# Turned squares of probabilities: sixteen SBUF-to-SBUF transfers, or four writes and one read through device memory

## The chip, the cores and the metric

One core of a Trainium2 chip. The time is the device time of one execution in microseconds (us), median of three runs. A core has a matrix engine (TensorE, in the profile PE, its weight loads PEld), a vector engine (VectorE, DVE), an activation engine (ScalarE, ACT), a general one (GpSimd, POOL), a queue engine that here only issues transfers (SyncE, SP), and 16 DMA engines that carry the transfers. Each engine works through its own instructions in order; semaphores order them against each other. SBUF is the on-chip memory of 128 partitions, PSUM the accumulator memory of TensorE, and device memory (DRAM in the code) lies off the core.

## The reference

Eight samples of 512 tokens with 512 features are normalised. One branch is a selective state-space scan, the other a gated feed-forward part whose gate is modulated by a causal attention of 16 heads of 32 numbers. What the change touches is the attention:

```python
q = (x @ Wq.T).reshape(b, s, H, HD)
k = (x @ Wk.T).reshape(b, s, H, HD)
v = (x @ Wv.T).reshape(b, s, H, HD)
scores = jnp.einsum('bqhd,bkhd->bhqk', q, k) / np.sqrt(HD)
scores = jnp.where(causal, scores, jnp.finfo(scores.dtype).min)
probs = jax.nn.softmax(scores, axis=-1)
out = jnp.einsum('bhqk,bkhd->bqhd', probs, v).reshape(b, s, d)
attn = out @ Wo.T
mod = MOD_SCALE * jnp.tanh(attn @ A)
gate_pre = h @ W_in_base.T + mod * (h @ A) @ B
...
x = x + s * g
```

`s` is the scan branch, `g` the silu of the feed-forward branch. Attention is used only through `attn @ A`, 16 numbers a token, so the kernel folds `Wv`, `Wo` and `A` into one matrix and gives every head 16 "values" plus a column of ones for the softmax's denominator.

## The kernel before

The kernel has two stages. The first, from the start to about 905 us, does the attention of all eight samples and, at its end, the convolutions of sample 0. The second does the scan, the feed-forward part and the projections; it is most of the time, and the change leaves it alone.

**Waves.** The attention goes in 32 waves: 8 samples times 4 groups of 4 heads. In the code a wave is `cur = (b, hg)`, the ones before are `prev`, `prev2`. A wave has four blocks of 128 queries, `qt` = 0 to 3, taken in the order 2, 1, 0, 3. Block `qt` sees `qt + 1` blocks of 128 keys.

**Steps of a block.** `scores` multiplies queries and keys into PSUM (line 1139, and the mask at 1144). `maxima` takes the row maxima on VectorE (1153). `exps` writes the exponentials to SBUF on ScalarE (1161). The product with the values needs the keys on the partitions, so the probabilities have to be turned. VectorE turns squares of 32 x 32 in place (`turn_blocks`, line 1180): blocks 0 to 2 go into the tile `ta` (128 x 4 x 6 x 128), block 3 into `tb` (128 x 4 x 4 x 128). Both have one buffer. After that every square is turned in itself, but still stands in the wrong block of 32 partitions.

**Moves.** `move_blocks` (1185) puts the squares in place: part (a, k) of `ta`, 32 partitions `a` and the column block `k`, goes to partitions `k` and column block `a` of `pta`; the same from `tb` to `ptb`. That is 16 transfers of 32 rows for each tile, issued by SyncE (1193). `pta` and `ptb` have one buffer each too.

**Products.** `attend` (1201, its matmuls at 1210) multiplies `pta` or `ptb` with the values into PSUM, and its `evict` copies the result to `o_sb`. `divide` turns it back on TensorE (1230) and divides by the denominator on VectorE. `modulation` closes a sample.

**What sets the order.** The kernel schedules by hand: each engine's order is the order in which the program issues. For the attention it is a string of words, one for a wave (1273). `S2`, `R2`, `E2` are scores, maxima and exponentials of block 2; `T2` turns it; `U3` turns block 3 of the wave before; `A` moves `ta` of this wave, `B` moves `tb` of the wave before; `a` and `e` are the products of the moved `ta` and `tb`, `O` the division; `q` and `k` are the projections of the next wave, `x`, `z`, `s`, `n`, `b`, `w`, `m` steps of the next sample (turning, values, statistics, normalising, weighing, modulation). A word with `>` is the eviction of the step with that letter. `ORDER_CONV` is for the last waves, in which `c` and `d` are convolutions of sample 0, and `ORDER_END` for the last. Behind the waves there is a tail, in which parts of the second stage (`run_part`) alternate with the last products.

**Other transfers on SyncE in this stage.** The loads of the next sample but one (`load_x`, 799, four at once), the store of the turned input (`scr_x`, 1069), constants in the first waves, and from the sixth wave before the end the weights of the convolutions (`load_win`, 218) and the stores of their results (`scr_c`, 259). GpSimd has its own queue: the row of normalising factors goes to device memory and back (979, 980), `hT` is stored (1089), the modulation is stored (1264).

Of the kernel before, what the change touches and what calls it, by code (L numbers as in the profile page):

```python
# [10 lines left out]
F32 = mybir.dt.float32  # L11
# [7 lines left out]
P = 128  # L19
# [4 lines left out]
TT = S // P  # L24
# [12 lines left out]
QD = 32  # L37
# [3 lines left out]
def mamba_gated_ffn_kernel(  # L41
# [22 lines left out]
    nc = tc.nc  # L64

    const = ctx.enter_context(tc.tile_pool(name="const", bufs=1))
    dram = ctx.enter_context(tc.tile_pool(name="scratch", bufs=1, space=DRAM))
# [6 lines left out]
    scr_c = [dram.tile([DI, S], F32, tag=f"scr_c{b}", name=f"scr_c{b}") for b in range(NB)]  # L74
    scr_r = [dram.tile([S], F32, tag=f"scr_r{b}", name=f"scr_r{b}") for b in range(NB)]
    scr_a = dram.tile([NS, DI], F32, tag="scr_a", name="scr_a")

    ident = const.tile([P, P], F32, tag="ident", name="ident")
    make_identity(nc, ident)
# [705 lines left out]
    with ExitStack() as c1:  # L785
# [53 lines left out]
        for i in range(2):  # L839
            z = wa.tile([P, TT, HG, 4, 2 * R], F32, tag=f"z{i}", name=f"z{i}")  # L840
# [344 lines left out]
        def move_blocks(b, hg, nm):  # L1185

            t = probs.pop((b, hg, nm))
            n = t.shape[2]
            to = pp.tile([P, 4, n, P], F32, tag=f"pt{nm}", name=f"pt{nm}_{b}_{hg}", bufs=1)
            for d in range(4):  # L1190
                for a in range(4):
                    k = (a + d) % 4
                    nc.sync.dma_start(to[ts(k, QD), a], t[ts(a, QD), k])  # L1193
            moved[b, hg, nm] = to

        PARTS = {
# [4 lines left out]
        def attend(b, hg, nm):  # L1201

            ps = bank(f"o_ps_{b}_{hg}_{nm}")
            t = moved.pop((b, hg, nm))
            steps = PARTS[nm]
            base = 0 if nm == "a" else (TT - 1) * P
            for s, (kt, qt, n, slot, by) in enumerate(steps):
                for h in range(4):
                    rhs = t[:, :, slot : slot + (n - 1) * by + 1 : by, ts(h, QD)]
                    nc.tensor.matmul(  # L1210
                        ps[ts(h, HD), qt * P - base : (qt + n) * P - base],
                        lhsT=zs[b % 2][:, kt, hg, h, :],
                        rhs=rhs.rearrange("p a n i -> p n a i"), start=(s == 0),
                        stop=(s == len(steps) - 1),
                    )

            def evict():
                if nm == "a":
                    outs[b, hg] = pp.tile([P, S], F32, tag="o_sb", name=f"o_{b}_{hg}", bufs=1)
                w = (TT - 1) * P if nm == "a" else P  # L1220
                nc.scalar.copy(outs[b, hg][:, base : base + w], ps[:, :w])

            return evict
# [24 lines left out]
        def modulation(b):  # L1248
# [22 lines left out]


        ORDER = (
            "S2 R2 U3 B E2 k s O x S1 k> R1 O> E1 x> T2 x a x> S0 a> R0 E0 T1 z z> "
            "T0 A z z> x x> b S3 R3 E3 q s b b e x q> s e> x> n b w m M"
        )
        ORDER_CONV = (
            "S2 R2 U3 B E2 d3 k O S1 d4 k> R1 O> E1 T2 c a c1 S0 a> R0 E0 c2 z z> T1 "
            "T0 A c3 z z> c4 S3 R3 E3 q d q> e d1 e> m w d2 M"
        )  # L1280
        ORDER_END = (
            "S2 R2 U3 B E2 d3 O S1 d4 R1 O> E1 T2 P a S0 a> R0 E0 P1 T1 T0 A S3 R3 E3 "
            "e 1 e> O O>"
        )

        def started(parts):
# [25 lines left out]
        def in_spare(fn, *args):  # L1312

            i = spare["n"] = spare.get("n", -1) + 1
            pair = ps_s.tile([P, 2, 512], F32, tag="s", name=f"s_spare_{i}")
            banks["special"] = lambda name: pair[:, 0, :]
            r = fn(*args)
            banks["special"] = None
            return r
# [15 lines left out]
            return [f for _, f in in_spare(started, sizes[i])]  # L1335

        items = [(b, hg) for b in range(NB) for hg in range(HG)]
        ends, late, divided = {}, {}, set()
        weigh_first()
        for g in range(len(items)):  # L1340
            cur = items[g]
            prev = items[g - 1] if g else None
            prev2 = items[g - 2] if g > 1 else None
            prev3 = items[g - 3] if g > 2 else None
            b, hg = cur
            n = b + 1
            ahead = items[g + 1] if g + 1 < len(items) else None
            todo = {k: [] for k in "bnxzsw"}
            if n < NB:
                if hg == 0:  # L1350
                    todo["b"], ends[n] = statistics(n)
                elif hg == 1:
                    todo["s"] = ends[n]
                    todo["n"] = [
                        lambda: [normalise(n, tt, nc.gpsimd) for tt in range(TT)]
                    ]
                elif hg == 2:
                    if n + 1 < NB:
                        load_x(n + 1)
                    todo["x"] = [lambda kt=kt: turn(n, kt) for kt in range(KT)]  # L1360
                    todo["w"] = [lambda: weigh(n)]
                else:
                    todo["z"] = [lambda tt=tt: values(n, tt) for tt in range(2)]
            if hg == 0 and b:
                todo["z"] = [lambda tt=tt: values(b, tt) for tt in (2, 3)]

            convs = g - (len(items) - 5)
            order = ORDER_CONV if convs >= 0 else ORDER
            if ahead is None:
                order = ORDER_END  # L1370
            open_, slot = {}, -1
            for w in order.split():
                kind, q = w[0], int(w[1]) if w[1:].isdigit() else None
                if kind == "S":
                    open_["R", q], open_["E", q] = scores(b, hg, q)
                    slot += 1
                elif kind in "RE":
                    open_.pop((kind, q))()
                elif kind == "T":
                    turn_blocks(*cur, q)  # L1380
                elif kind == "U":
                    if prev:
                        turn_blocks(*prev, q)
                elif w == "A":
                    move_blocks(*cur, "a")
                elif w == "B":
                    if prev:
                        move_blocks(*prev, "b")
                elif w in ("a", "e"):
                    if prev:  # L1390
                        late[w] = attend(*prev, "a" if w == "a" else "b")
                elif w in ("q", "k"):
                    late[w] = query_key(*ahead, w)
                    if w == "q" and g == len(items) - 6:
                        load_xn(0)
                        for d in range(3):
                            load_win(0, d)
                elif w == "O":
                    of = prev2 if prev2 not in divided else prev
                    if of:  # L1400
                        divided.add(of)
                        late["O"] = divide(*of)
                elif w == "m":
                    if prev2 and prev2[1] == HG - 1:
                        late["M"] = modulation(prev2[0])
                elif w == "M":
                    if "M" in late:
                        late.pop("M")()
                elif kind in "cd" and len(w) == 1:
                    late[kind] = convolution(2 * convs + (kind == "d"))  # L1410
                elif kind in "cd":
                    if late.get(kind):
                        late[kind].pop(0)()
                elif w == "P":
                    late["P"] = step_of_time(0)
                elif w == "P1":
                    for f in late["P"]:
                        f()
                elif w == "1":
                    late["P"] = step_of_time(1)  # L1420
                elif w[1:] == ">":
                    if w[0] in late:
                        late.pop(w[0])()
                elif todo.get(w):
                    f = todo[w].pop(0)()
                    if w in "xz":
                        late[w] = f
                if kind == "E" and g == 0:
                    for f, *i in folds[slot]:
                        f(*i)  # L1430
                if kind == "E" and (b, hg, slot) in const_steps:
                    const_steps[b, hg, slot]()
            if g == 0:
                for tt in range(TT):
                    values(0, tt)()
            assert not any(todo.values()), todo


        last = items[-1]
# [3 lines left out]
            f()  # L1443
        state["wait"] = True
        banks["second"] = None
        evict = in_spare(attend, *last, "a")
        run_part()
        evict()
        for i in (2, 3, 4):
            for f in step_of_time(i):  # L1450
                f()
# [41 lines left out]
    for b in range(NB):  # L1493
# [6 lines left out]
        for s in range(STEPS):  # L1500
            k = b * STEPS + s
# [107 lines left out]
```

## Time and profile before

| what | us |
|---|---|
| median of three runs | 3203.05 (3201.35 to 3204.26) |
| the profiled execution, its time | 3203.12 |
| its span, first to last instruction | 3201.3 |
| PE busy in the span | 2993.1 |
| DVE busy | 2517.0 |
| POOL busy | 1977.2 |
| ACT busy | 1266.6 |

The mean granted clock of TensorE is 0.96. The page also cuts the span into 40 slices of 80 us; a digit is the busy share in tenths, for PEclk the granted clock in tenths, for DMA the mean share of the 16 DMA engines.

```profile
PE 8677877779799999999999999999999999999999
...
DVE 5455654556669998997998899889879988998885
...
PEclk9788988889899999999999999999999999999999
DMA 4555555555567878787978877787778788787974
```

The first eleven digits are the attention stage: PE is mostly at six to eight tenths and its clock below full, DVE at about half, the DMA engines at about half. In the remaining 29 PE is at nine tenths or more.

How the page is read: a group of instructions has its source line, engine, operation, output and input tiles and count, then busy time and the mean of one, then the idle time before it with what ended it. PE's ends are modelled. Who waited for whom is inferred from semaphores. "SPq" is SyncE's queue of issuing instructions, which isn't counted as an engine's busy time. A DMA packet is one contiguous row of a transfer, and each DMA engine that took part adds a packet of 4 bytes that counts the transfer's semaphore up.

### The profile page before, as it was taken

Reading aid. Unit: us, or ns where it says so; the run is one execution under the profiler, and the core shown is the slowest. Engines: PE = TensorE matmul, PEld = TensorE weight load, DVE = VectorE, ACT = ScalarE, POOL = GpSimd, SP = SyncE. Lnnn points to the kernel's source line nnn. Section 1 sums busy time; section 2 is a strip of 40 time slices with the busy share of each in tenths; the row PEclk is TensorE's granted clock in tenths of the full one; section 3 lists DMA queues with packets and bytes.
Section 4 is the critical chain, followed back from the end, with each engine's and each line's share of the span. In section 5 each row is a group of like instructions: output and inputs, shape, how many; then the busy total and the mean of one; then the engine's idle time right before and its main releaser. Section 6 shows DMA issues by size and latency. Waiting matters only on the chain.

```text
span 3201.3 us, 35722 instructions
## 1 busy us (share of the span) xinstructions
PE 2993.1 (93%) x11956; PEld 1301.3 (41%) x11956; DVE 2517.0 (79%) x2858; ACT 1266.6 (40%) x2224; POOL 1977.2 (62%) x924
## 2 busy tenths in 40 slices
PE   8677877779799999999999999999999999999999
PEld 5333443334343344344434443443444344434444
DVE  5455654556669998997998899889879988998885
ACT  4343443434334443433443334334334433443432
POOL 2321122121058887887777787777778787788885
PEclk9788988889899999999999999999999999999999
DMA  4555555555567878787978877787778788787974
GB/s 145 140 130 131 138 150 142 125 133 162 164 181 207 204 208 227 206 206 185 243 181 217 214 202 199 200 228 200 197 194 226 191 222 207 198 207 186 232 187 120
DMA packets 344905, 595.13 MB, mean 186 GB/s; under 512 B 44749, under 2 KB 176333, under 8 KB 340116
## 3 DMA queue, kind: packets, MB, share of 16 engines
q1 hardware_dynamic: 338528, 576.35, 69.6%
q0 software_dynamic: 2192, 10.50, 1.1%
q10 hardware_dynamic: 4004, 6.01, 0.8%
q8 instruction: 96, 1.57, 0.2%
q14 instruction: 85, 0.70, 0.1%
HBM read 466.04 MB, written 42.77 MB: 159 GB/s over the span
## 4 chain that ended last, share of the span: by engine, by line
PE 79%; SPq 9%; DVE 4%; DMA 4%; POOL 2%; issue 2%; ACT 1%; DVEq 0%; ACTq 0%; POOLq 0%
PE ps_gu L298 27%; PE ps_acc L360 14%; PE ps_in L206 12%; SPq L1193 9%; PE y L685 7%; PE ps_out L389 7%; PE s L1139 2%; PE ps_q L1117 1%; PE ps_k L1117 1%; POOL xn L1048 1%; DMA scr_r<-rs 1%; PE ps_gu L309 1%; PE o_ps_a L1210 1%; DMA pta<-ta 1%; PE ps_p L482 1%
## 5 line engine op out<-in xcount | busy, mean ns | idle before, releaser
L673 POOL TENSOR_TENSOR x<-x,cc 128x1024 f32<-128x1024 f32 x512 | 1206.6, 2364 | 467.2 <-DVE x L668 447.9
L668 DVE TENSOR_TENSOR_SCAN x<-decay,x 128x512 f32<-128x512 f32 x1024 | 1210.9, 1211 | 3.4 <-ACT decay L646 3.1
L646 ACT ACTIVATE decay<-dt,an 128x511 f32<-128x511 f32 x1024 | 694.7, 687 | 632.5 <-DVE x L668 615.8
L298 PE MATMUL ps_gu<-ht,wgu 128*128 128x512 f32 x2048 | 915.4, 598 | 0.8 <-DVE mod_t L1263 0.8
L662 POOL TENSOR_TENSOR x<-x,bb 128x1024 f32<-128x1024 f32 x256 | 607.5, 2373 | 6.8 <-DMA wgu<-in_w_ffn 5.7
L298 PEld LDWEIGHTS ps_gu<-ht,wgu 128*128 128x128 f32 x2048 | 382.0, 190 | 522.2 <-issue 478.1
L360 PE MATMUL ps_acc<-m,wd 128*128 128x512 f32 x1024 | 449.2, 595 | 0.0
L206 PE MATMUL ps_in<-xnt,win 128*128 128x512 f32 x960 | 430.0, 594 | 0.0
L1153 DVE TENSOR_REDUCE mx<-s 128x2 f32<-128x768 f32 (+3 forms) x256 | 198.5, 817 | 272.9 <-PE s L1144 271.9
L1161 ACT ACTIVATE p<-s,mx 128x128 f32<-128x128 f32 (+3 forms) x512 | 228.4, 528 | 319.5 <-DVE mx L1153 319.5
L660 DVE TENSOR_TENSOR x<-x,dtb_ps 128x1024 f32<-128x1024 f32 x255 | 305.3, 1197 | 1.1 <-ACT dtb_ps L657 0.6
L360 PEld LDWEIGHTS ps_acc<-m,wd 128*128 128x128 f32 x1024 | 192.0, 190 | 256.1 <-issue 249.8
L206 PEld LDWEIGHTS ps_in<-xnt,win 128*128 128x128 f32 x960 | 179.4, 190 | 227.0 <-issue 222.0
L685 PE MATMUL y<-x,sel 128*32 128x512 f32 x2048 | 251.7, 598 | 3.3 <-POOL x L673 3.3
L389 PE MATMUL ps_out<-xc,wout 128*128 128x512 f32 x496 | 219.4, 594 | 0.0
L979 POOL DMA_DIRECT2D scr_r<-rs x7 | 5.5, 784 | 323.4 <-DVE rs L962 323.4
L245 DVE SCALAR_TENSOR_TENSOR conv<-ps_in,cw,conv 128x511 f32<-128x511 f32 x168 | 125.3, 746 | 47.3 <-ACT conv L264 43.3
L1139 PE MATMUL s<-k,q 32*128 32x384 f32 (+3 forms) x1024 | 139.6, 556 | 19.3 <-ACT p L1161 17.4
L389 PEld LDWEIGHTS ps_out<-xc,wout 128*128 128x128 f32 x496 | 92.7, 190 | 118.8 <-issue 118.8
L685 PEld LDWEIGHTS y<-x,sel 128*32 128x32 f32 x2048 | 54.5, 109 | 181.5 <-issue 146.4
L282 ACT ACTIVATE zth<-ps_in 128x512 f32<-128x512 f32 x64 | 38.2, 597 | 223.3 <-PE ps_in L206 223.3
L1117 PE MATMUL ps_q<-xrT,wq 128*128 128x512 f32 x248 | 124.6, 649 | 0.0
(216 smaller groups left out, 2305.3 us busy)
## 6 DMA issues: line engine op xcount, KB each, us to landing
x<-scr_c SPq DMA_DIRECT2D x512, 512.0 KB
wgu<-in_w_ffn SPq DMA_DIRECT2D x256, 256.0 KB
pta<-ta SPq DMA_DIRECT2D x512, 96.0 KB
ptb<-tb SPq DMA_DIRECT2D x512, 64.0 KB
win<-in_w_in SPq DMA_DIRECT2D x128, 256.0 KB
wd<-in_w_ffn SPq DMA_DIRECT2D x128, 256.0 KB
scr_c<-xc SPq DMA_DIRECT2D x64, 256.0 KB
wout<-in_out_w SPq DMA_DIRECT2D x64, 256.0 KB
```

The costliest lines, as they stand in the source:

```text
L206: nc.tensor.matmul(ps, lhsT=w[:, kt, :], rhs=xnt[b][:, kt, :], start=(kt == 0), stop=(kt == KT - 1))
L298: nc.tensor.matmul(st[i, which], lhsT=w[:, kt, :], rhs=ht[b][:, kt, :], start=(kt == 0), stop=(kt == KT - 1 and (which == 1 or i == 3)),)
L360: nc.tensor.matmul(st["acc"], lhsT=w[:, j, :], rhs=mlp[b, f], start=(f == 0), stop=(f == NF - 1))
L389: nc.tensor.matmul(st["ps"], lhsT=w[:, d % 4, :], rhs=xc[b, d], start=(d == 0), stop=(d == ND - 1),)
L646: nc.scalar.activation(decay[n][:, 1:], spread[b][2][:, 1:], AF.Exp, scale=an[:, g // 4, g % 4 : g % 4 + 1])
L660: nc.vector.tensor_tensor(t, t, by.unsqueeze(1).to_broadcast([P, 2, S]), ALU.mult)
L662: nc.gpsimd.tensor_tensor(t, t, spread[b][0].unsqueeze(1).to_broadcast([P, 2, S]), ALU.mult)
L668: nc.vector.tensor_tensor_scan(t, decay[n], t, 0.0, ALU.mult, ALU.add)
L673: nc.gpsimd.tensor_tensor(t, t, spread[b][1].unsqueeze(1).to_broadcast([P, 2, S]), ALU.mult)
L685: nc.tensor.matmul(y[ts(j, QD), :], lhsT=sel[:, i0 + n, :], rhs=xs[k - 3 + j][:, n, :], start=(i0 + n == 0), stop=(i0 + n == 3),)
L1161: nc.scalar.activation(pr["t"][:, :, :, h, :].rearrange("p b k i -> p k b i"), sc[h // 2][:, h % 2, :w].rearrange("p (k b i) -> p k b i", ...
L1193: nc.sync.dma_start(to[ts(k, QD), a], t[ts(a, QD), k])
```

## The change

Two scratch tensors in device memory for each kind of square, used in turn by the parity of the head group, of shape (column block `k` 4, partition in the block `j` 32, partition block `a` 4, `n` blocks of 128 numbers). For each `k` a transfer writes column block `k` of all 128 partitions of `ta` (or `tb`) into them; then one transfer reads the whole of it, where (`k`, `j`) are the partitions and (`a`, `n`) the columns. Each row written is 768 or 512 numbers long, each row read 3072 or 2048.

```diff
+    scr_t = {
+        (nm, i): dram.tile([4, QD, 4, n, P], F32, tag=f"scr_t{nm}{i}", name=f"scr_t{nm}{i}")
+        for nm, n in (("a", 6), ("b", TT)) for i in range(2)
+    }
...
-            for d in range(4):
-                for a in range(4):
-                    k = (a + d) % 4
-                    nc.sync.dma_start(to[ts(k, QD), a], t[ts(a, QD), k])
+            d = scr_t[nm, hg % 2]
+            for k in range(4):
+                nc.sync.dma_start(d[k].rearrange("j a n c -> a j (n c)"), t[:, k])
+            nc.sync.dma_start(to, d.rearrange("k j a n c -> (k j) a n c"))
             moved[b, hg, nm] = to
```

The order of the words changes with it. `a` still uses the wave before, but stands behind `A`; `e` uses the wave before that one and stands behind `B`; `O` comes after `e`; the tail takes the product of `tb` and the division of the last wave but one.

```diff
         ORDER = (
-            "S2 R2 U3 B E2 k s O x S1 k> R1 O> E1 x> T2 x a x> S0 a> R0 E0 T1 z z> "
-            "T0 A z z> x x> b S3 R3 E3 q s b b e x q> s e> x> n b w m M"
+            "S2 R2 U3 B e E2 k e> s S1 k> R1 E1 O x T2 O> x> x x> z z> S0 R0 E0 T1 T0 A a z z> "
+            "x x> a> b S3 R3 E3 q s b b x q> x> s n b w m M"
         )
         ORDER_CONV = (
-            "S2 R2 U3 B E2 d3 k O S1 d4 k> R1 O> E1 T2 c a c1 S0 a> R0 E0 c2 z z> T1 "
-            "T0 A c3 z z> c4 S3 R3 E3 q d q> e d1 e> m w d2 M"
+            "S2 R2 U3 B e E2 d3 k e> S1 d4 k> R1 E1 O c T2 O> c1 z z> S0 R0 E0 c2 T1 T0 A "
+            "a z z> c3 a> c4 S3 R3 E3 q d q> d1 m w d2 M"
         )
         ORDER_END = (
-            "S2 R2 U3 B E2 d3 O S1 d4 R1 O> E1 T2 P a S0 a> R0 E0 P1 T1 T0 A S3 R3 E3 "
-            "e 1 e> O O>"
+            "S2 R2 U3 B e E2 d3 e> O S1 d4 R1 E1 T2 O> P S0 R0 E0 P1 T1 T0 A a a> S3 R3 E3 "
+            "1"
         )
...
                 elif w in ("a", "e"):
-                    if prev:
-                        late[w] = attend(*prev, "a" if w == "a" else "b")
+                    of = prev if w == "a" else prev2
+                    if of:
+                        late[w] = attend(*of, "a" if w == "a" else "b")
...
                 elif w == "O":
-                    of = prev2 if prev2 not in divided else prev
-                    if of:
-                        divided.add(of)
-                        late["O"] = divide(*of)
+                    if prev2:
+                        late["O"] = divide(*prev2)
...
         banks["second"] = None
-        evict = in_spare(attend, *last, "a")
+        in_spare(attend, *items[-2], "b")()
         run_part()
-        evict()
+        in_spare(divide, *items[-2])()
+        in_spare(attend, *last, "a")()
```

More of the change, by code (lines that the diff above doesn't have):

```diff
@@ L1337, in mamba_gated_ffn_kernel @@
         items = [(b, hg) for b in range(NB) for hg in range(HG)]
-        ends, late, divided = {}, {}, set()
+        ends, late = {}, {}
         weigh_first()
```

## Prediction

> **What bounds the kernel now.** I read the page's chain of waits first, to see whether the copies that the change touches are on the path at all.
>
> ```profile
> PE 79%; SPq 9%; DVE 4%; DMA 4%; POOL 2%; issue 2%; ACT 1%; DVEq 0%; ACTq 0%; POOLq 0%
> ```
>
> These are shares of the 3201.3 us span by what the chain ran through. SPq, SyncE's queue, holds 9%, and the chain's row by line gives the same 9%, 288 us, to line 1193, the copies of the turned squares. Next, that line's own instructions, and SyncE's order of work (start, length, both in us).
>
> ```profile
> L1193 SPq DMA_DIRECT2D pta<-ta x512: 507/590/5876, 42.9 to 877.9; - x171
> L1193 SPq DMA_DIRECT2D ptb<-tb x512: 507/589/1867, 59.6 to 888.2; - x171
> ```
>
> ```profile
> 341.76 12.25 SPq L1193 DMA_DIRECT2D pta<-ta  x16
> 354.13 10.86 SPq L1193 DMA_DIRECT2D ptb<-tb  x16
> 365.10 10.05 SPq L1193 DMA_DIRECT2D pta<-ta  x16
> 375.57 10.97 SPq L1193 DMA_DIRECT2D ptb<-tb  x16
> ```
>
> An issue takes 0.59 us, 0.63 with the gap to the next. Thirty-two a wave are 20 us of issuing, and SyncE goes from one group to the next almost without a pause. Then the busy times of two stretches (length, PE, PEld, DVE, ACT, POOL, clock, DMA share, GB/s): the whole attention stage, and its quickest wave.
>
> ```profile
> 42.92:878.57 835.65, 644.93 (x4572) 337.12 (x4570) 467.33 (x617) 342.61 (x773) 161.66 (x128) 0.85 0.56 140
> 145.39:163.53 18.14, 18.14 (x153) 10.31 (x149) 15.96 (x22) 9.52 (x24) 0.00 (x0) 1.00 0.42 102
> ```
>
> No engine fills the stage: PE has 645 of 836 us at a granted clock of 0.85. The quickest wave takes 18.1 us with PE full; the mean, from the first group of wave 0 at 42.92 to that of wave 31 at 867.66, is 824.7 / 31 = 26.6 us. So the issue of the copies does cost time, and a cure for it could bring at most those 288 us. What counts is whether the new transfers are a cure.
>
> **The change, part by part.** Removed: 32 copies a wave, 20 us of SyncE. Added: eight writes and two reads, 10 x 0.63 = 6.3 us of SyncE. That would be 14 us less, if SyncE were only issuing.
>
> Added, a wait: a read can't be issued before its four writes have landed, and it waits on SyncE, which works in order. Behind it stand the next square's four writes, the loads of x (line 799), the store of scr_x (line 1069), and in the last five waves the loads of win and the stores of scr_c. DVE waits too: the next wave's first transpose into ta or tb (line 1180) must wait until the writes out of it have landed, and behind that transpose stand the next maxima, so ACT's exponentials and PE's next scores. So the writes' landing sets the wave, if it takes long.
>
> How long depends on how many DMA engines a write uses. The trace of before has no such write: its source has 128 rows, its destination's outermost axis has 4 (then 32, then a run of 768 or 512 numbers). What it does show is a transfer of 33 rows, alone on ACT's queue, in the window from 1087 to 1092.5 us (packets, MB, share of 16 engines):
>
> ```profile
> q10 hardware_dynamic: 44, 0.07, 5.6%
> ...
> scr_p<-parts_p ACTq DMA_DIRECT2D x1, 66.0 KB
> ```
>
> It has 44 packets: 33 rows and 11 completions. The moves of 32 rows have 16 completions each (the next window: 787 packets, 512 of them rows, 275 over, which is 16 each and a few of the group before). So a transfer is cut into equal lots of whole outermost entries, 11 lots of 3 rows there. An outermost axis of 4 gives at most four lots, so I take **four engines** for each new write, and the same four each time. For both steps no row is direct. Bounds: 4 and 16 engines.
>
> The Trainium skill speaks against the change more plainly. "DMA: Bandwidth & Descriptors", section "Rules for kernel authors", says that an outermost axis smaller than 16 on either side confines the whole transfer to that many engines, and its section on why a DMA increments its semaphore by 16 adds that on SyncE's queue these are the lowest-numbered ones. The 11 agrees; that the smaller side decides, and which engines, no row here shows. By the rule the sum is the four-engine one below, by the source's 128 rows the sixteen-engine one.
>
> Now the price of a packet. Three windows: 16 moves from ta, some 15 from tb, and a store of 1 MB to device memory.
>
> ```profile
> q1 hardware_dynamic: 787, 1.57, 63.1%
> ...
> pta<-ta SPq DMA_DIRECT2D x16, 96.0 KB
> ```
>
> ```profile
> q1 hardware_dynamic: 709, 1.01, 39.2%
> ```
>
> ```profile
> q0 software_dynamic: 142, 1.05, 41.4%
> ...
> scr_x<-xnT POOLq DMA_DIRECT2D x1, 1024.0 KB, 5.0
> ```
>
> Engine time is share x 16 x window. First: 0.631 x 16 x 10.4 = 105 us for 512 rows of 3 KB and 275 completions; with a few ns for each completion, 0.200 us a row. Second: 0.392 x 16 x 10.6 = 66.5 us for 469 rows of 2 KB, 0.137 each. Third: 0.414 x 16 x 6.5 = 43.1 us for 128 rows of 8 KB, 0.336 each, so by bytes 0.126 for 3 KB and 0.084 for 2 KB. The moves are dearer for each byte than the store by 1.6. The new write reads 32-partition blocks side by side, as the moves do, and lands in device memory, as the store does. I take two thirds of the way from the store to the moves, since the slower side of a packet sets it: 0.175 and 0.119.
>
> Each write has 128 rows, four writes 512, on four engines 128 packets each:
> - writes of square a: 128 x 0.175 = 22.4 us (16.1 to 25.6)
> - writes of square b: 128 x 0.119 = 15.2 us (10.8 to 17.5)
> - reads, 128 rows of 12 KB and of 8 KB on 16 engines: 8 x 0.504 + 8 x 0.336 = 6.7 us, on the same four queues between the writes
> - two gaps, in which SyncE waits for a landing and then issues the read. The nearest row is the small transfer of line 1264:
>
> ```profile
> DMA to landing us min/median/max: 2.1/3.0/6.1
> ```
>
>   With 0.63 for the issue, 2.7 to 3.6 each: 6 us a wave (5.5 to 7.3).
>
> The wave is then 22.4 + 15.2 + 6.7 + 6 = **50.3 us** (39.1 to 57.1), against 26.6: 31 x 23.7 = 735 us more (388 to 946).
>
> Moved: the product of square a (32 matmuls of line 1210) now uses the wave before and stands right after its own wave's copies have been issued; that of b moves a wave later, the division with it. I cost these at nothing on PE: the same matmuls run, and the cover is a whole wave between issue and use. Gone, that cover would cost a wait as at the end of the stage before:
>
> ```profile
> 880.19 2.79 PE L1210 MATMUL s_spare<-pta,z 128*32 128x256 f32 x32 [6.91 <-DMA pta<-ta]
> ...
> 892.86 1.08 PE L1210 MATMUL s_spare<-ptb,z 128*32 128x128 f32 x32
> ```
>
> There no next wave covers. Before, the last product of b began 25 us after the last group from ta was issued (867.66). Now: 22.4 + 3.6 + 4 (read of a) + 15.2 + 3.6 + 2.7 + 2.1 = 54 us. PE has only two parts of the next stage in between, 4 us each and there before too, so I add 25 us (10 to 30). The product of b for wave 30 and its division, added here, are 1.9 us, and leave the loop.
>
> POOL's transfers (lines 979, 980, 1089, 1264) are on their own queue but the same DMA engines; their waits are inside a wave that PE, DVE and ACT then leave half empty. The stage after 905 us isn't touched.
>
> Sum: the profiled execution is 3203.1 us by its own clock, 1.8 around its span, and the median of the runs 3203.05, so the two can stand for each other. 3203 + 735 + 25 = 3963, say **3960 us**.
>
> **Rivals.** *All sixteen engines* (the source's 128 rows decide, or each write takes another four). Then a wave's transfers are 32 x (0.126 to 0.200) + 32 x (0.084 to 0.137) + 6.7 + 6 = 19 to 24 us. For it: nothing in the trace shows a transfer with unlike outermost axes. Against: the 33-row row. The wave goes to 22.3 us, 31 x 4.3 = 133 less: 3070 us; bounds from a wave of 18.1 (2940) to one of 25 (3153). The point from which it decides is a wave of transfers under 26.6 us, some nine engines.
>
> *Nothing gained.* Sixteen engines, but SyncE, held 19 to 24 us a wave by the two landings, is as full as it was with 20 us of issuing: 3203 us. For it: the chain charges SyncE, and the wait takes the issue's place. Against: a wave has more slack than before for its products.
>
> *Four engines at the store's price.* If the blocks don't hinder each other the wave is 39.1 us: 3203 + 388 + 10 = 3600. It is the forecast's cheap end, and the moves' price its dear one: 3203 + 946 + 30 = 4180.
>
> **How the numbers follow.** Four engines 0.83 (the forecast, with both its ends), sixteen 0.14, nothing gained 0.03. The time is the likeliest's, 3960. The range leaves the faster rival out: with 0.14 to 0.17 there, it has to hold nearly all of the four-engine case, 3540 to 4220. Runs of before lie within 0.1%, so 0.2% is about what can be told from no change: faster 0.15, same 0.02, slower 0.83.
>
> **What would show it.** Right: in a window holding only writes, four completions for each beside 128 rows, a DMA share near a quarter while SyncE waits, waves of 40 to 57 us, DVE's transposes waiting for the writes to scr_t, PE at under half in the stage, and everything after it as before. Wrong: sixteen completions for each write, then a share over a half and waves under 25 us. The size is wrong if the packets of 3 KB are near 0.126 or over 0.2 us.

## The result and the profile after

The changed kernel takes 3715.6 us (median of four runs, 3711.9 to 3717.7) against 3203.2: 1.160 times the time before, 95% interval 1.158 to 1.162, or 512 us more. Its profiled span is 3714.0 us. All of the difference lies in the attention stage: the first group of copies of wave 0 still starts at 42.8 us, the first of wave 31 at 1360.6 instead of 867.7. A wave takes (1360.6 - 42.8) / 31 = 42.5 us instead of 26.6, which is 31 x 15.9 = 493 us, and from there to the last product of `b` it is 43 us instead of 25.

The page's chain of waits of the kernel after, by engine and by line:

```profile
PE 65%; DMA 27%; SPq 3%; DVE 3%; ACT 1%; issue 1%; POOL 0%; DVEq 0%; ACTq 0%; POOLq 0%
PE ps_gu L302 23%; DMA scr_ta<-ta 17%; PE ps_acc L364 12%; PE ps_in L210 11%; PE y L689 6%; PE ps_out L393 6%; DMA scr_tb<-tb 5%; DMA pta<-scr_ta 4%; SPq L1196 2%; PE o_ps_a L1214 1%; PE ps_gu L313 1%; PE s L1143 1%; DVE mx L1157 1%; PE ps_p L486 1%; PE ps_z L1099 1%
```

SyncE's own 9% has gone to 3%: its issuing isn't the limit any more. In its place stand the transfers themselves, 27%, of which 17% are the writes out of `ta` and 5% those out of `tb`. The slices of the page for PE and its clock show the stage stretched, and PE in it at about half, where it was mostly at six to eight tenths:

```profile
PE   7355555555555549999999999999999999999999
...
PEclk8677777777777869999999999999999999999999
```

One wave as SyncE's queue saw it (start, length of the issue, us):

```profile
360.66 6.32 SPq L1196 DMA_DIRECT2D scr_ta<-ta  x4
381.07 0.33 SPq L1197 DMA_DIRECT2D pta<-scr_ta  x1
381.44 5.97 SPq L1196 DMA_DIRECT2D scr_tb<-tb  x4
398.23 0.33 SPq L1197 DMA_DIRECT2D ptb<-scr_tb  x1
```

Four writes are issued in 6 us; then the queue stands for 11 to 14 us until they have landed, and only then the read goes out. From the first write of `ta` to its read it is 20.4 us, from the first write of `tb` to its read 16.8. These two follow each other without a gap and make the wave. PE's products and DVE's transposes wait for them (us in all, times, longest):

```profile
PE o_ps_a L1214 <- DMA pta<-scr_ta: 331.2, 29, 21.1
...
DVE ta L1184 <- DMA scr_ta<-ta: 222.9, 27, 17.7
```

What the DMA engines do meanwhile shows from 382 to 398 us, while `tb` is written. The rows are the share in tenths and the rate in 40 slices; the last line is SyncE's queue with packets, MB and share.

```profile
DMA  9569989899561222222422222222222222222210
GB/s 276 123 215 369 430 369 430 369 492 369 215 246 36 77 102 102 102 102 102 143 102 102 102 102 102 102 102 102 102 102 102 102 102 102 102 102 102 102 72 10
...
q1 hardware_dynamic: 672, 2.62, 44.2%
```

First the read of `a` runs on all engines at 370 to 430 GB/s. Then the writes run on a flat 102 GB/s at a quarter of the share: four of sixteen engines, by which each moves 25.5 GB/s. The packets say the same: 672 are 512 rows of four writes, 128 rows of the read, and 32 completions, 16 for the read and 4 for each write.

### The profile page after: what moved, and what is told of

The parts are those of the page before. It is cut to its first block, busy times and chain, and to the rows that moved or that the text cites. A ratio compares the mean times of both kernels' runs of the same rounds, so it can differ in the third digit from the quotient of the medians.

```text
span 3714.0 us, 34730 instructions
## 1 busy us (share of the span) xinstructions
PE 3060.3 (82%) x11956; PEld 1331.2 (36%) x11956; DVE 2516.1 (68%) x2858; ACT 1265.7 (34%) x2224; POOL 1977.1 (53%) x924
## 4 chain that ended last, share of the span: by engine, by line
PE 65%; DMA 27%; SPq 3%; DVE 3%; ACT 1%; issue 1%; POOL 0%; DVEq 0%; ACTq 0%; POOLq 0%
PE ps_gu L302 23%; DMA scr_ta<-ta 17%; PE ps_acc L364 12%; PE ps_in L210 11%; PE y L689 6%; PE ps_out L393 6%; DMA scr_tb<-tb 5%; DMA pta<-scr_ta 4%; SPq L1196 2%; PE o_ps_a L1214 1%; PE ps_gu L313 1%; PE s L1143 1%; DVE mx L1157 1%; PE ps_p L486 1%; PE ps_z L1099 1%
## 5 line engine op out<-in xcount | busy, mean ns | idle before, releaser
L1214 PE MATMUL o_ps_a<-pta,z 128*32 128x256 f32 x992 | 85.1, 520 | 331.2 <-DMA pta<-scr_ta 331.2
L1184 DVE STREAM_TRANSPOSE ta<-p 128x1536 f32<-128x1536 f32 (+2 forms) x96 | 115.4, 1228 | 242.6 <-DMA scr_ta<-ta 222.9
L1214 PEld LDWEIGHTS o_ps_a<-pta,z 128*32 128x32 f32 x992 | 45.8, 165 | 362.4 <-issue 249.6
L1090 POOL TENSOR_SCALAR xnT<-xrT,ln 128x512 f32<-128x512 f32 x28 | 43.3, 1555 | 231.4 <-DMA scr_x<-xnT 231.4
L1214 PE MATMUL o_ps_b<-ptb,z 128*32 128x128 f32 x960 | 54.4, 400 | 122.9 <-DMA ptb<-scr_tb 122.8
```

## The experiments

Theory F: a write is confined to as many DMA engines as its outermost axis has entries, four, and they are the same four each time. Its rivals are named with the runs. Ratios are to the kernel before on the same chip; runs without an interval were timed once. The words "wave" and its length are taken as above, from the first group of wave 0 to that of wave 31.

**e1: the same bytes, outermost axis 32.** Each write takes 32 rows of all four column blocks.

```diff
-            for k in range(4):
-                nc.sync.dma_start(d[k].rearrange("j a n c -> a j (n c)"), t[:, k])
+            rows = d.rearrange("k j a n c -> a j k (n c)")
+            for i in range(4):
+                nc.sync.dma_start(rows[i], t[ts(i, QD)].rearrange("p k n c -> p k (n c)"))
```

> Same bytes, same number of transfers (four writes, one read for each square), same order of the words; but each write takes 32 rows of all four column blocks, so that its outermost axis is 32 and not 4. Theory F (a write is confined to as many DMA engines as its outermost axis has entries, the same four each time): 16 completions for each write, 32 packets an engine and square; wave 21 to 25 us, whole kernel 3090 to 3215 us, likeliest 3120. Rival R (the trip through device memory with two landings awaited on SyncE costs the time, whatever the engines): 3650 us or more.

Measured: 3194.95 us, ratio 0.997 (0.996 to 0.998). Number of transfers, bytes, waits and order are those of the change; only how the same rows are dealt to the four writes differs, and with it the outermost axis, and 520 us are gone. From 357 to 367 us, with the read of `a` first and then the four writes of `tb`:

```profile
GB/s 442 49 197 147 246 344 492 295 492 393 344 295 344 344 393 295 295 246 344 344 230 377 352 393 410 402 402 393 410 385 287 115 49 49 57 25 8 0 0 0
...
q1 hardware_dynamic: 720, 2.62, 74.7%
```

The 720 packets are 512 rows of the writes, 128 rows of the read and 80 completions, 16 for each of the five transfers, and the rate is near 400 GB/s where the changed kernel's writes had 102. F holds, R falls. The time came out at the dear end of what F allowed. The stage in one line (length, then PE, PEld, DVE, ACT, POOL, clock, DMA share, GB/s):

```profile
42.90:870.00 827.10, 633.19 (x4570) 327.77 (x4569) 464.64 (x622) 339.27 (x773) 161.62 (x128) 0.87 0.76 240
```

The DMA engines are at 0.76 of their time at 240 GB/s, where they were at 0.56 and 140 before the change: every byte now moves twice. A wave is 26.4 us, hardly less than before.

**e2: outermost axis 2.** Each write is cut into two halves of 64 rows.

```diff
             for k in range(4):
-                nc.sync.dma_start(d[k].rearrange("j a n c -> a j (n c)"), t[:, k])
+                to_k = d[k].rearrange("j a n c -> a j (n c)")
+                for i in range(2):
+                    nc.sync.dma_start(to_k[ts(i, 2)], t[ts(i, 2 * QD), k])
```

> Each write is cut in two halves of 64 rows, outermost axis 2. Theory F: two engines for each, always the same two, 256 packets each for a square: 31 us for a, 21.5 us for b, wave 41.1 + 15.5 + 10.8 = 67 us, whole kernel about 4550 us. If the engines rotated from write to write: near 3750. Rival R: only eight more issues a wave, 5 us, so at most 3870.

Measured: 4528.6 us. In a window in which only `tb` is written (716 to 730 us):

```profile
GB/s 53 53 47 59 47 53 53 47 53 53 47 53 53 47 59 47 53 53 47 53 53 47 59 47 47 59 47 53 53 47 53 53 47 59 47 47 59 47 53 53
...
q1 hardware_dynamic: 360, 0.72, 13.2%
```

Half the rate of the four-engine writes, and an eighth of the full share: two engines. Eight writes follow each other, and the rate stays that of two. The queue doesn't serve them one at a time either: in the packet records a completion at 717.21 us is followed by the next write's row within 10 ns, before the other engine's completion at 717.31. Had the writes gone to different engines, their rates would have added up. So the engines are the same each time, and the count follows the axis.

**e3: the new order alone,** with the sixteen moves inside SBUF of before.

```diff
-            d = scr_t[nm, hg % 2]
-            for k in range(4):
-                nc.sync.dma_start(d[k].rearrange("j a n c -> a j (n c)"), t[:, k])
-            nc.sync.dma_start(to, d.rearrange("k j a n c -> (k j) a n c"))
+            for d in range(4):
+                for a in range(4):
+                    k = (a + d) % 4
+                    nc.sync.dma_start(to[ts(k, QD), a], t[ts(a, QD), k])
```

> The sixteen SBUF moves for each square as before the change, in the new order of the words (products one phase later). Theory F: the order isn't the cost; SyncE still issues 32 copies, 20.3 us a wave, and the product waits on landings (50 us in the stage) go: 3100 to 3200 us. Rival O (the new order itself costs, since pta and ptb are held longer and the products stand elsewhere): 3300 us or more.

Measured: 3161.4 us, ratio 0.987 (0.985 to 0.989). The order isn't the cost; by itself it saves 43 us. It is also 34 us better than e1 (same chip): once all engines take part, the trip through device memory is still no better than the 32 moves.

**e4: sixteen writes of 32 rows each** and one read for a square.

```diff
             for k in range(4):
-                nc.sync.dma_start(d[k].rearrange("j a n c -> a j (n c)"), t[:, k])
+                to_k = d[k].rearrange("j a n c -> a j (n c)")
+                for i in range(4):
+                    nc.sync.dma_start(to_k[i], t[ts(i, QD), k])
```

> Sixteen writes of 32 rows each for a square (outermost axis 32) and one read: the bytes and the scratch layout of the change, four times its writes. Theory F: sixteen engines, so the 17 issues of 0.63 us set it: 10.8 us and a landing of 2.3 us for each square, wave 26 to 29 us, 3240 to 3350 us, faster than the change although it issues more. Rival R: more issues on the same trip, 3715 us or more.

Measured: 3312.5 us. Four times the writes of the change, and 403 us faster than it. SyncE's queue over a square of `tb` and one of `ta`:

```profile
301.53 12.37 SPq L1198 DMA_DIRECT2D scr_tb<-tb  x16
315.34 0.34 SPq L1199 DMA_DIRECT2D ptb<-scr_tb  x1
315.73 15.71 SPq L1198 DMA_DIRECT2D scr_ta<-ta  x16
333.01 0.34 SPq L1199 DMA_DIRECT2D pta<-scr_ta  x1
```

The reads go out 1.4 and 1.6 us after the last write's issue, where the changed kernel stood for 11 to 14. With sixteen engines the writes land almost as they are issued, and their issue takes most of the time, 12.4 of 13.8 us and 15.7 of 17.3, as F has it.

**e5: e1's transfers in the old order.** The edit is the kernel before with `scr_t` and the transfers of e1.

> The transfers of e1 (through device memory, sixteen engines), in the order of the words before the change, so that the product of b stands at the end of the wave and that of a before the scores of block 0. Theory L (the new order's worth is to hide the landing of the read, 8 to 10 us after its issue in e1): 3230 to 3330 us, with PE waiting 100 us or more for the reads. If the order doesn't matter: 3195 within 10.

Measured: 3254.7 us, ratio 1.016 (1.015 to 1.018). PE's wait for the read of `a`, first in e5, then in e1 (us in all, times, longest):

```profile
PE o_ps_a L1215 <- DMA pta<-scr_ta: 86.3, 17, 7.6
```

```profile
PE o_ps_a L1215 <- DMA pta<-scr_ta: 47.0, 16, 6.4
```

By the ratios the new order is worth 1.9% with this trip, some 60 us, against 1.3% with the moves; on e1's chain the read of `a` lands 6.7 to 9.7 us after its issue, and the product has to be kept away from it. The wait itself came out under the 100 us that I had put down; the rest of the 60 us I didn't trace.

**e6: e1 with the read on GpSimd's queue.**

```diff
-            nc.sync.dma_start(to, d.rearrange("k j a n c -> (k j) a n c"))
+            nc.gpsimd.dma_start(to, d.rearrange("k j a n c -> (k j) a n c"))
```

> e1 with the read issued on GpSimd's queue, so that SyncE no longer stands at the landing of the writes (410 us in e1). Theory W (that stand, with the next square's writes behind it, is what keeps e1 at 3195): 3100 to 3170 us. Rival B (the doubled bytes, 240 GB/s at a DMA share of 0.76 in the stage, keep it there): 3180 to 3210; if GpSimd's own work gets stuck behind the landings, up to 3260.

Measured: 3255.5 us, ratio 1.017 (1.015 to 1.018): slower than e1, near the last case of the expectation. The stand at the landing only moved to another queue with work behind it. From the view of waits of GpSimd and of PE (us in all, times, longest):

```profile
POOL pta L1198 <- DMA scr_ta<-ta: 206.3, 18, 18.6
```

```profile
PE ps_x L1065 <- POOL xn L1052: 104.9, 28, 18.2
```

GpSimd stands 206 us for the writes out of `ta`, 116 for those out of `tb`, its normalising comes late, and PE waits 105 us for it, where it waited 43 in e1. Whether e1's remaining time is the doubled bytes or the landings isn't settled by this.

**e7: e3, with the squares that stay on their partitions copied by GpSimd.** Four of the sixteen squares of a tile, a = k, don't change partitions.

```diff
-            for d in range(4):
+            for d in range(1, 4):
                 for a in range(4):
                     k = (a + d) % 4
                     nc.sync.dma_start(to[ts(k, QD), a], t[ts(a, QD), k])
+            for a in range(4):
+                nc.gpsimd.tensor_copy(to[ts(a, QD), a], t[ts(a, QD), a])
```

> e3 (moves inside SBUF, new order), but the four squares of each tile that stay on their own partitions are copied by GpSimd: 24 issues a wave on SyncE, 15.2 us, in place of 32 and 20.3. Theory I (SyncE's issuing sets the wave in e3, 40% of its chain): 5 us a wave less at most, 3161 - 31 x (1.5 to 4) = 3040 to 3115 us. Rival P (PE at a lowered clock and the chain through scores, maxima and exponentials set it): 3145 to 3170.

Measured: 3115.5 us, ratio 0.973 (0.971 to 0.974), the fastest of all the kernels here, 87 us under the kernel before on the same chip and 600 under the change. At 3115 the gain stands on the edge of what theory I gave, and outside rival P. SyncE's queue, nearly without a pause in the kernel before, now has gaps:

```profile
324.02 8.33 SPq L1197 DMA_DIRECT2D ptb<-tb  x12
332.52 7.50 SPq L1197 DMA_DIRECT2D pta<-ta  x12
343.00 8.67 SPq L1197 DMA_DIRECT2D ptb<-tb  x12
```

From 332.52 + 7.50 = 340.0 to 343.0 it issues nothing. The copies cost GpSimd 0.82 and 0.61 us each, 5.7 us a wave. The run takes a quarter of the moved bytes off the DMA engines together with a quarter of the issues, so it doesn't tell the two apart.

**e8: e3, with the moves of `tb` issued by GpSimd.**

```diff
+            queue = nc.sync if nm == "a" else nc.gpsimd
             for d in range(4):
                 for a in range(4):
                     k = (a + d) % 4
-                    nc.sync.dma_start(to[ts(k, QD), a], t[ts(a, QD), k])
+                    queue.dma_start(to[ts(k, QD), a], t[ts(a, QD), k])
```

> e3 with the moves of b issued on GpSimd's queue: 16 issues a wave on SyncE, 10.2 us. Theory I: 3040 to 3130 us, if GpSimd's issues (0.5 to 0.8 us each, about 10 us a wave) don't hold up its normalising. Rival P: 3145 to 3170; if GpSimd becomes the bound, over 3170.

Measured: 3197.9 us, ratio 0.999 (0.998 to 1.000), 37 us over e3. GpSimd's group for these issues (busy, mean ns, idle before, releasers):

```profile
L1198 POOL DMA_DIRECT2D ptb<-tb x487 | 239.1, 499 | 216.1 <-DVE stats L952 89.2 <-DVE tb L1184 59.3 <-PE ps_k L1121 23.0
```

Sixteen issues of 0.5 us and the stand before the first one, 216 us in the stage, lie in front of GpSimd's own work. Half of SyncE's issuing was taken away, and a new bound came with it: in the chain from 60 to 860 us GpSimd's issues hold 9.9% and SyncE's 7.1%, where SyncE's held 40% in e3. So this run doesn't decide between theory I and rival P.

## Why the prediction was right, and where its size was off

It said slower, by the writes' four engines, at 3960 us in a range from 3540 to 4220; it is slower, by that mechanism, at 3715.6. Step by step:

- **SyncE's issuing bounds the stage before.** Right in the main: the issues hold 40% of e3's chain, and e7 takes eight of the 32 off and is 46 us faster than e3. But e3 gains 43 us with all 32 issues in place, so the order of the work had a share in it too. "At most 288 us" was never reached; the best here is 87.
- **Four engines, the same each time.** Right, both halves. Four completions for a write, the plateau at 102 GB/s, e1 with 32 entries and 16 completions, and e2, whose 4550 us, worked out before the run, met 4528.6. Of two readings of the 33-row transfer, the source's 128 rows or the smaller outermost axis, the smaller axis decides, as the Trainium skill has it ("DMA: Bandwidth & Descriptors", "Rules for kernel authors"). That it is the same few engines every time, which its section on the semaphore's 16 states, is now shown too (e2); which ones, no run shows. DVE waited for the writes as forecast, 223 us; PE is busy for 0.53 of the stage where I had said under half.
- **The price of a packet: the step that was mis-sized.** I took 0.175 us for 3 KB and 0.119 for 2 KB, two thirds of the way from the store to the moves. By the same method, share x 16 x window, from 405 to 417 us (only `ta` being written) and from 386.5 to 396 (`tb`, and the last five rows of the read of `a`):

```profile
q1 hardware_dynamic: 419, 1.25, 25.7%
```

```profile
q1 hardware_dynamic: 463, 0.95, 26.0%
```

  0.257 x 16 x 12 = 49.3 us for 407 rows and 12 completions is 0.121 us a row. 0.260 x 16 x 9.5 = 39.5 us holds 22 completions, five rows of 12 KB at 0.53 us by their packet records, and 436 rows of 2 KB, which leaves 0.084 for each of these. That is the store's price, my cheap end. Writes are then 128 x 0.121 + 128 x 0.084 = 26.2 us a wave, not 37.6. My reason for going two thirds of the way to the moves' price, that the writes read blocks of 32 partitions side by side as the moves do, was wrong: in e1 sixteen engines read the same blocks as the moves, and the median row of 3 KB still takes 0.121 us (mean 0.160, from 60 to 870 us), where the moves' took 0.20 in the mean. That the slower side of a packet sets its time, no run here shows.
- **Reads and gaps** came out larger: 42.5 - 26.2 = 16.3 us a wave against 12.7. In the wave shown above, one of the quickest, 37.9 us from its first write of `ta` at 360.66 to the next group's at 398.60, they are 11.7. Other waves have more: 19.2 us in place of 16.8 for `tb` where the store of scr_x goes first (341.13 to 360.29), and 27.3 in place of 20.4 for `ta` where the stall described at the end falls in (436.94 to 464.26). The first wave, with the loads of the constants, takes 65.6. These I had costed at nothing.
- **The two misses** pull apart: the writes 11.4 us a wave too dear, the rest 3.6 too cheap. The range held because its cheap end was the store's price; of the cases named, *four engines at the store's price*, 3600 us, is the nearest.
- **Readings that were off, too little to matter.** The first window of moves held 531 rows and 256 completions, not 512 and 275, and each window some rows of the other size: by the packet records 0.20 and 0.13 us a row where I had 0.200 and 0.137. And the point from which *all sixteen engines* decides lies, at my own prices, at 4 x 37.6 / (26.6 - 12.7), some eleven engines, not nine.
- **The products one phase later** I had costed at nothing. The same matmuls run, but the move itself is a gain of 43 us, which e3 shows alone. In the changed kernel PE waits 331 us for the reads of `a` in spite of it; no run has its four-engine writes in the old order, so what the move is worth there is open.
- **The tail.** 43 us from the last group of `ta` to the last product of `b`, against 25: 18 more, where I had put 54 on that path and added 25.

The terms account for the whole: with the measured 42.5 for the wave and 18 for the tail, the sum becomes 3203 + 31 x 15.9 + 18 = 3714.

The rival *all sixteen engines* had a premise that this change doesn't meet, and its size was wrong as well: e1 is that case, and it is 3195, not 3070, outside its bounds on the dear side. By that sum it would have run at 22.3 us a wave; with the DMA engines at 240 GB/s and two landings awaited in a queue it ran at 26.4, and which of the two holds it there is open. The rival *nothing gained* is nearer to what sixteen engines give.

## What to carry to other kernels

Before a transfer is re-cut, look at the outermost axis of both of its sides. Here four entries beside 128 rows gave four DMA engines, two beside 64 gave two, 32 on both sides sixteen, and 33 rows only eleven. For a transfer on SyncE's or ACT's queue, the completions beside its rows told the number in the profile. Fewer and larger transfers gained little by being fewer: against the kernel before, four writes on four engines lost 512 us, sixteen smaller ones on sixteen engines 108, and four on sixteen engines gained 9, which is 0.3%. e6 shows that a wait for a landing holds up whatever stands behind it on its new queue; a queue with nothing behind it wasn't tried. Work that needn't be a transfer at all, here the squares that stay where they are, was the cheapest to take off the queue.

## What the runs showed of the hardware that I hadn't expected

While a small transfer from GpSimd's queue is under way, the others slow down, in the changed kernel nearly to a stop. Once a sample it writes 2 KB to device memory as 512 single numbers (line 983 after the change). It was issued at 437.5 us; from 443 to 449 all queues together moved this:

```profile
DMA packets 22, 0.05 MB, mean 8 GB/s; under 512 B 6, under 2 KB 6, under 8 KB 22
```

In the 12 us from 405 to 417 the same four engines moved 419 packets, so about 200 would have gone through in 6. The next sample shows the same from 608 to 614 us with 32 packets. In the kernel before the drop is smaller: in the same stretch, 5.5 to 11.5 us after its issue, the rate is 26 to 51 GB/s in six samples, lowest after the issue at 389.0, where it had been 115 to 153 in the 4 us before the issue. In the changed kernel the transfer takes 10.3 to 14.0 us to land, before 8.8 to 11.5. That it is the cause is inferred from the times; no run was made without it.

A read whose rows lie in one piece takes SyncE 0.33 us to issue, a write of the change with its three axes 0.56 to 0.72 (medians; the shortest 0.50), though both have 128 rows.
